# A conditioned transformer block: larger first transfers, QKV tokens by GpSimd's queue, statistics three products sooner, variances rooted later

## The chip, the cores and the metric

The kernel runs on one core of a Trainium2 chip. The metric is device time in microseconds for one execution. A core has five engines that run side by side, each through its own instructions in order: TensorE (PE) multiplies matrices, VectorE (DVE) and ScalarE (ACT) work element by element, GpSimd (POOL) does the same more slowly, and SyncE (SP) issues transfers. Transfers between main memory and the on-chip memory SBUF can be issued by SP, ACT or GpSimd. TensorE writes to PSUM, a small memory in banks.

## The reference

The block takes two rows of 2,048 tokens, 512 wide, and one condition vector for each row.

```
mod = silu(condition) @ Wada + bada          # six vectors of 512 per row
sh_a, sc_a, gt_a, sh_m, sc_m, gt_m = split(mod, 6)
xm = layernorm(x, g1, be1) * (1 + sc_a) + sh_a
q, k, v = split(xm @ Wqkv)                    # 16 heads of 32
x = x + gt_a * (softmax(causal(q k^T / sqrt(32))) v @ Wproj + bproj)
xm = layernorm(x, g2, be2) * (1 + sc_m) + sh_m
x = x + gt_m * (gelu(xm @ W1 + b1) @ W2 + b2) # hidden width 2,048
```

All of it is in 32-bit floating point.

## The kernel before

**Stages.** `dit_block_kernel` works in this order: a first stage (loads, the first modulation, the first normalized tokens); the query, key and value products of row 0 (`Qkv.run`); attention of row 0 (`attention_phase`); its output projection (`project_phase`), in which the first group of row 1 is prepared (`between`); then the same for row 1; last the MLP for both rows.

**First stage.** The condition and the scale and bias vectors (g1, be1, g2, be2, b1, b2) are loaded as rows of one tile `rows`, by ACT's queue, seven small transfers. SP's queue loads the first 512 tokens as four transfers of 256 KB (`Qkv.load_x`), two sixths of Wada as eight of 256 KB (`load_wada`), the query and key weights as four of 512 KB (`load_w`, tile `wqk`), and then the value weights (`load_wv`). TensorE transposes `rows`, and DVE copies the result to `cols`. A token's mean and variance come from DVE (`stats`, lines 216 to 221); `inv_std` turns the variances of four tiles into 1/sqrt and shift by a square root on ACT and two small operations on DVE. ACT scales the tokens in place (`scaled`, line 964), TensorE transposes them, four 128x128 blocks to a PSUM bank (line 214, tile `ps_xt`), and DVE and ACT apply the modulation on the way out of PSUM (`transposed`, result `xmT`). The modulation itself, silu(condition) @ Wada, is the matmul into `ps_mod` (`modulation`).

**Products with fewer multiplications.** Queries, keys and values are computed in groups of 512 tokens, g = 0 to 3. A product of 2 x 2 blocks is formed with seven block products in place of eight; `unit` orders them. For that, sums of weight blocks (`weight_sum`, line 944, on GpSimd in row 0) and sums of token blocks (`token_sum`, line 997, on DVE) are formed ahead. The first unit of row 0 (`plain`, tile `ps_qk`) goes without, while the weight sums are being formed. Each unit's results leave PSUM (six banks `mm`) by ACT (line 1059, 1130) and DVE (lines 1072, 1078, 1134), are split into a high and a low part (lines 1064, 1066), and are stored for attention.

**Steps inside a group.** `Qkv.run` counts 42 steps n in each group, one for each product, and prepares group g+1 at fixed steps: at n = 3 its tokens are loaded if they are not yet; at n = 10 to 13 their statistics; at 15 and 25 the scaling; at 18 and 28 the transposes; at 36 to 40 the token sums. At n = 30 the tokens of group g+2 are loaded. Between the products the first scores of attention are computed, their maxima taken by DVE (lines 498 and 504, tiles `junk`, `mx`). 

```
if n == 30 and g + 2 < NG:
    self.load_x(g + 2)
if 10 <= n < 10 + MTT and g + 1 > row.b:
    self.stats(g + 1, n - 10)
```

**MLP weights.** During both QKV stages GpSimd also forms the block sums of the MLP weights (`Pieces`, line 1253) in parts of SBUF that attention does not use yet, and stores them to main memory by its own queue (line 1273, `w1d`, `w2d`).

**What sets the order.** TensorE's instructions, and those wrapped in `act(...)` or given `keep`, keep the order of the program on their engine. All others are placed by the framework's scheduler, which may move them ahead or back on their engine by its own estimate of when their inputs are ready. Once placed, an engine executes strictly in that order. A tile with `bufs=N` has N buffers in turn: a load into it waits until the last reader of the buffer's former content is done. The transfers issued by GpSimd stand in its instruction order, among its sums.

Of the kernel before, what the change touches and what calls it, by code (L numbers as in the profile page):

```python
# [17 lines left out]
P = 128  # L18
# [9 lines left out]
def dit_block_kernel(  # L28
# [104 lines left out]


    first = const.tile([P, 1], F32, tag="first", name="first")
    nc.scalar.activation(first, eps, AF.Sqrt)


    cols = const.tile([P, 64], F32, tag="cols", name="cols")
# [60 lines left out]
    def x_rows(n):  # L200
        t0 = (n % NT) * P
        return x[n // NT, t0 : t0 + P, :]
# [695 lines left out]
    class Qkv:  # L898
# [13 lines left out]
                for n in (S1, S2, A22)  # L912
            }

        def load_x(self, g):
            xts = []
            for t in range(MTT):
                xt = self.qp.tile([P, D], F32, tag="x", name="x", bufs=4)
                nc.sync.dma_start(xt, x_rows(self.row.b * NT + g * MTT + t))
                xts.append(xt)  # L920
            self.xts[g] = xts

        def load_w(self, queue):
# [214 lines left out]
        def run(self, hp, also, early=()):  # L1138
# [3 lines left out]
            for g in range(NG):  # L1142
                at = [0]

                def tick():
# [1 line left out]
                    if n >= self.STEPS:  # L1147
                        return
                    if n == 30 and g + 2 < NG:
                        self.load_x(g + 2)  # L1150
                    if g + 1 < NG:
                        if n == 3 and g + 1 not in self.xts:
                            self.load_x(g + 1)
                        if 10 <= n < 10 + MTT and g + 1 > row.b:
                            self.stats(g + 1, n - 10)
                        if n in (15, 25):
                            self.scaled(g + 1, n // 25)
                        if n in (18, 28):
# [138 lines left out]
    def project_phase(row, psum, between):  # L1297
# [5 lines left out]
        with pool(f"proj{b}") as pp:  # L1303
# [14 lines left out]
            for k, i in enumerate(last_order):  # L1318
# [6 lines left out]
                for t in range(TQ):  # L1325
# [28 lines left out]
                        )  # L1354
                    between(n)
                    n += 1
        lo, hi = b * NT, (b + 1) * NT
        inv_std(mv2, rstd2, shift2, lo, hi)


    row = Row(0)
    with pool("wada") as wp, pool("qkv0") as qp, pool("hl0") as hp, pool(
        "ps_qkv0", bufs=6, space=PSUM
    ) as ps_mm:
        rows = wp.tile([n_rows, P], F32, tag="rows", name="rows")
        for r, n, src in (
            (0, n_cond, cond.rearrange("b (c p) -> (b c) p", p=P)),
            (r_g1, C, g1.rearrange("(c p) -> c p", p=P)),
            (r_be1, C, be1.rearrange("(c p) -> c p", p=P)),
            (r_g2, C, g2.rearrange("(c p) -> c p", p=P)),  # L1370
            (r_be2, C, be2.rearrange("(c p) -> c p", p=P)),
            (r_b1, FC, b1.rearrange("(c p) -> c p", p=P)),
            (r_b2, C, b2.rearrange("(c p) -> c p", p=P)),
        ):
            nc.scalar.dma_start(rows[r : r + n, :], src)
        wada_v = Wada.rearrange("(c p) f -> p c f", p=P)
        wada = {}

        def load_wada(s0, s1):
            w = row.vv[:, NT - 2 * C :].rearrange("p (n c) d -> p n c d", n=2)  # L1380
            if s0 % 3 == 2:
                mr = modr
            else:
                mr = wp.tile([P, D], F32, tag="mr", name="mr")
                nc.gpsimd.memset(mr, 0.0)
            for n, s in enumerate((s0, s1)):
                nc.gpsimd.dma_start(
                    mr[n * HD : n * HD + B, :],
                    bada[s * D : (s + 1) * D].partition_broadcast(B),
                )  # L1390
            for k in range(C):
                for n, s in enumerate((s0, s1)):
                    nc.sync.dma_start(w[:, n, k, :], wada_v[:, k, s * D : (s + 1) * D])
            wada[s0] = w, mr

        qkv = Qkv(row, qp, ps_mm)
        qkv.load_x(0)
        load_wada(0, 1)
        qkv.load_w(nc.sync)
        qkv.load_wv(hp, nc.sync)  # L1400

        ps_c = ps_mm.tile([P, n_rows], F32, tag="mm", name="ps_c")
        transpose(ps_c, rows)
        nc.vector.tensor_copy(cols[:, :n_rows], ps_c)
        sc = wp.tile([P, C, HD], F32, tag="sc", name="sc")
        nc.vector.memset(sc, 0.0)

        def modulation(s0):
# [7 lines left out]
            for k in range(C // 2):  # L1416
                for half in range(2):
                    for n in range(2):
                        at = (2 * half + n) * HD
                        kk = half * C // 2 + k  # L1420
                        mm(
                            ps[at : at + HD, :], sc[:, kk, :], w[:, n, kk, :],
                            start=(k == 0), stop=(k == C // 2 - 1),
# [18 lines left out]
        def scale_shift(a, c, r_g, r_be, shift, scale):  # L1442
# [6 lines left out]
                )  # L1449
            nc.vector.tensor_tensor(c, c, mod[:, shift], ALU.add)  # L1450

        for t in range(MTT):
            qkv.stats(0, t)
        halves = [qkv.norm(0, 0, True)]

        act(
            nc.scalar.activation(
                sc[:, :, :B], col(0, n_cond).rearrange("p (b c) -> p c b", c=C), AF.Silu
            )
        )  # L1460
# [15 lines left out]
        def also(g, n):  # L1476
# [52 lines left out]
    with pool("qkv1") as qp, pool("ps_qkv1", bufs=6, space=PSUM) as ps_mm:  # L1529
# [799 lines left out]
```

## Time and profile before

| | before |
|---|---|
| median of 3 runs | 2249.56 us (2248.82 to 2253.02) |
| profiled execution | 2252.46 us |
| its span | 2250.7 us |
| TensorE busy | 2210.1 us, 98% |
| VectorE busy | 1537.3 us, 68% |
| GpSimd busy | 1298.3 us, 58% |
| ScalarE busy | 1003.6 us, 45% |
| granted TensorE clock, mean | 0.999 of full speed |

The span reaches from the first to the last recorded instruction. Busy shares are averages over stages; the places that matter are found in the timeline, where an instruction's idle time before it and what released it stand in brackets. L206 is the one line through which every matmul goes, and L214 that of every transpose, so the stage is told by the tiles: `ps_qk` and `ps_a`, `ps_b`, `ps_c` are the QKV products, `ps_xt` the transposes of tokens, `s` the scores.

### The profile page before, as it was taken

What the parts mean: (1) busy time and instruction counts of PE and PEld (TensorE: products, weight loads), DVE (VectorE), ACT (ScalarE), POOL (GpSimd) and SP (SyncE); (2) the same over time, 40 slices, a digit from 0 to 9 for tenths busy, and PEclk for the clock granted to TensorE, in tenths of its full rate; (3) what the DMA queues carried; (4) which work ended last, traced back from release to release, by engine and by line L of the source; (5) the groups of instructions that cost most, each with busy time, mean ns of one, the idle gap of its engine ahead of it and who ended that gap; (6) DMA issues with size and microseconds to landing.
All of it is one profiled execution on the core that took longest, in us unless ns stands there. A gap on an engine that the chain in (4) does not pass through costs nothing.

```text
span 2250.7 us, 33467 instructions
## 1 busy us (share of the span) xinstructions
PE 2210.1 (98%) x12057; PEld 1429.4 (64%) x12057; DVE 1537.3 (68%) x3309; ACT 1003.6 (45%) x2012; POOL 1298.3 (58%) x807
## 2 busy tenths in 40 slices
PE   7999999999999999999999999999999999999998
PEld 5887555555543588855555555345787787688687
DVE  4678766777757667777677767663685585576576
ACT  4434555555564253365665556614322422331410
POOL 4253998998983696299989898444105204304210
PEclk9999999999999999999999999999999999999999
DMA  8787142231324799532324113363353354353433
GB/s 274 247 277 193 44 92 70 62 85 48 107 96 135 247 308 321 152 83 67 80 67 104 48 46 131 108 233 127 114 174 131 125 182 147 106 187 126 159 126 109
DMA packets 160510, 311.57 MB, mean 138 GB/s; under 512 B 16544, under 2 KB 48844, under 8 KB 158552
## 3 DMA queue, kind: packets, MB, share of 16 engines
q1 hardware_dynamic: 155488, 285.53, 41.8%
q0 software_dynamic: 4480, 23.36, 2.7%
q8 instruction: 95, 1.56, 0.3%
q14 instruction: 71, 0.58, 0.1%
q10 hardware_dynamic: 376, 0.55, 0.1%
HBM read 229.95 MB, written 87.29 MB: 141 GB/s over the span
## 4 chain that ended last, share of the span: by engine, by line
PE 88%; DVE 4%; POOL 3%; DMA 2%; ACT 1%; issue 1%; SPq 0%; DVEq 0%; ACTq 0%; POOLq 0%
PE ps_a L206 26%; PE st L206 18%; PE ps_b L206 12%; PE o L206 10%; PE s L206 9%; PE ps_c L206 4%; PE sm L206 3%; PE ps_o L206 3%; DVE junk L498 1%; POOL ee L695 1%; PE ps_xt L214 1%; ACT e L670 1%; DVE mx L504 1%; PE ps_o L214 1%; DVE stat L218 1%
## 5 line engine op out<-in xcount | busy, mean ns | idle before, releaser
L670 ACT ACTIVATE e<-st 128x512 f32<-128x512 f32 (+1 forms) x1152 | 575.1, 579 | 362.6 <-PE st L206 319.2
L504 DVE TENSOR_REDUCE mx<-s 128x1 f32<-128x512 f32 x576 | 381.6, 686 | 193.4 <-PE s L206 192.4
L695 POOL TENSOR_TENSOR ee<-ee,e 128x2048 f32<-128x2048 f32 x106 | 485.8, 4583 | 10.4 <-ACT e L670 4.4
L206 PE MATMUL st<-qst,kst 128*128 128x512 f32 (+3 forms) x1280 | 408.8, 386 | 0.0
L206 PE MATMUL s<-kst,qst 128*128 128x512 f32 (+3 forms) x1046 | 380.5, 395 | 6.1 <-DVE mx L504 3.7
L206 PE MATMUL ps_a<-sum,w 128*128 128x256 f32 (+1 forms) x1088 | 328.7, 431 | 0.1
L206 PE MATMUL o<-e,vv 128*32 128x512 f32 (+3 forms) x2560 | 293.2, 537 | 0.3 <-POOL e L682 0.3
L206 PEld LDWEIGHTS st<-qst,kst 128*128 128x128 f32 x1280 | 228.5, 188 | 97.7 <-issue 66.0
L498 DVE CUSTOM_DVE_ANT_0 junk<-s,causal 128x128 bf16<-128x128 f32 (+3 forms) x470 | 220.7, 470 | 61.0 <-PE s L206 47.0
L1797 POOL TENSOR_TENSOR sum<-w 128x256 f32<-128x256 f32 x30 | 22.1, 738 | 395.2 <-PE ps_a L206 263.8
L206 PEld LDWEIGHTS s<-kst,qst 128*128 128x128 f32 x1046 | 194.9, 188 | 71.1 <-DVE mx L504 17.0
L206 PEld LDWEIGHTS ps_a<-sum,w 128*128 128x128 f32 x1088 | 204.5, 190 | 40.1 <-issue 11.4
L695 POOL TENSOR_TENSOR ee<-e 128x2048 f32<-128x2048 f32 x42 | 192.5, 4583 | 43.2 <-ACT e L670 42.3
L206 PEld LDWEIGHTS <-sel 32*128 32x128 bf16 x1152 | 29.5, 91 | 197.0 <-issue 196.1
L2016 ACT ACTIVATE h<-h,cols 128x512 f32<-128x512 f32 x120 | 76.8, 711 | 136.0 <-DVE h L1718 136.0
L504 DVE TENSOR_REDUCE mx<-st 128x1 f32<-128x512 f32 x192 | 131.0, 683 | 0.6
L682 POOL TENSOR_SCALAR_AFFINE_SELECT e<-e 128x512 f32<-128x512 f32 x128 | 83.3, 669 | 67.6 <-ACT e L670 67.5
L206 PE MATMUL st<-fold,sel 32*128 32x512 bf16 (+1 forms) x1152 | 117.5, 372 | 1.3
L206 PEld LDWEIGHTS o<-e,vv 128*32 128x32 f32 x2560 | 59.1, 108 | 92.4 <-issue 73.0
L1718 DVE TENSOR_TENSOR h<-c,ps_b 128x256 f32<-128x256 f32 x90 | 37.9, 421 | 103.5 <-PE ps_b L206 103.0
L1066 POOL TENSOR_TENSOR lo<-lo,hi 128x512 fp32r<-128x512 f32 x32 | 40.6, 1274 | 103.9 <-ACT hi L1064 102.0
L206 PE MATMUL ps_b<-sum,w 128*128 128x256 f32 (+1 forms) x384 | 95.0, 383 | 0.0
(237 smaller groups left out, 3590.2 us busy)
## 6 DMA issues: line engine op xcount, KB each, us to landing
qst<-q SPq DMA_DIRECT2D x128, 256.0 KB
kst<-k SPq DMA_DIRECT2D x128, 256.0 KB
w<-w1d SPq DMA_DIRECT2D x32, 896.0 KB
w<-w2d SPq DMA_DIRECT2D x28, 1024.0 KB
w<-w2d SPq DMA_DIRECT2D x28, 768.0 KB
q<-hi SPq DMA_DIRECT2D x32, 256.0 KB
q<-lo SPq DMA_DIRECT2D x32, 256.0 KB
k<-hi SPq DMA_DIRECT2D x32, 256.0 KB
```

Source lines behind the costliest of these rows:

```text
L206: return tc.keep_in_program_order(nc.tensor.matmul(*args, **kw))
L214: return tc.keep_in_program_order(nc.tensor.transpose(dst, src, ident[:n, :n]))
L218: ins = nc.vector.bn_stats(st, xt)
L498: nc.vector.tensor_tensor_reduce(junk[:, :w], x, causal[:, QB - w :], 1.0, MASKED, ALU.add, ALU.max, m,)
L504: self.vector(nc.vector.tensor_reduce(m, x, axis=AX.X, op=ALU.max))
L670: act(nc.scalar.activation(e4[:, h, :w], sts[h][:, :w], AF.Exp))
L682: nc.gpsimd.affine_select(d, d, pattern=[[0, HC], [1, P]], compare_op=ALU.is_ge, fill=0.0, base=0, channel_multiplier=-1,)
L695: act(nc.gpsimd.tensor_tensor(dst, x, y, ALU.add))
L1066: engine.tensor_tensor(lo, d, hi.bitcast(F32), ALU.subtract)
L1718: act(nc.vector.tensor_tensor(dst, x, y, ALU.add))
L1797: act(engine.tensor_tensor(dst, u, v, op))
L2016: nc.scalar.activation(d[j], d[j], AF.Gelu, bias=col(r_b1 + half * HF + fs[j], 1))
```

## The change

1. The first transfers. Tokens come in pairs of tiles, two transfers of 512 KB for a group in place of four of 256 KB, in two buffers of a pair each in place of four. Two sixths of Wada come as four transfers of 512 KB in place of eight, each with two neighbouring 128-row blocks, and the product takes the blocks in a matching order. `rows` is split: condition, g1 and be1 are loaded first, by ACT's queue; the other four vectors by SP at step 22 of group 0 (`load_other_rows`), and are transposed and copied at step 20 of group 1 (`other_columns`). Row 0's second group of tokens is issued by SP ahead of the value weights, where it was issued at step 3.
2. The first stage's order. The first square root of a constant, which called up ACT's table, is replaced by a Silu there and a square root behind the Silu of the condition. TensorE executes 6 and 24 transposes of the identity whose result is not used (`busy`). The statistics and the scaling come after the Silu; the modulation is computed ahead of the first transposes.
3. In both rows the tokens of group g+2 are issued at step 30 by GpSimd, in place of SP.
4. The statistics of group g+1 start at step 7 in place of 10 and the first scaling at step 12 in place of 15, for g = 1 and 2; g = 0 keeps 10 and 15. Where g equals the row's number, the statistics now keep program order.
5. Row 0's square root for the second normalization, over 16 tiles, leaves the end of `project_phase` and is called at step 16 of group 0 of row 1. Row 1 keeps it in `project_phase`.

```diff
-    nc.scalar.activation(first, eps, AF.Sqrt)
...
-        def load_x(self, g):
+        def load_x(self, g, queue=nc.sync):
             xts = []
-            for t in range(MTT):
-                xt = self.qp.tile([P, D], F32, tag="x", name="x", bufs=4)
-                nc.sync.dma_start(xt, x_rows(self.row.b * NT + g * MTT + t))
-                xts.append(xt)
+            for t in range(0, MTT, 2):
+                xt = self.qp.tile([P, 2, D], F32, tag="x", name="x", bufs=2)
+                t0 = (g * MTT + t) * P
+                queue.dma_start(
+                    xt,
+                    x[self.row.b, t0 : t0 + 2 * P, :].rearrange("(n p) d -> p n d", p=P),
+                )
+                xts += [xt[:, n, :] for n in range(2)]
             self.xts[g] = xts
...
                     if n == 30 and g + 2 < NG:
-                        self.load_x(g + 2)
+                        self.load_x(g + 2, nc.gpsimd)
...
-                        if 10 <= n < 10 + MTT and g + 1 > row.b:
-                            self.stats(g + 1, n - 10)
-                        if n in (15, 25):
+                        s0 = 7 if g else 10
+                        if s0 <= n < s0 + MTT and g + 1 > row.b:
+                            self.stats(g + 1, n - s0, row.b == g)
+                        if n in (s0 + 5, 25):
                             self.scaled(g + 1, n // 25)
...
-        lo, hi = b * NT, (b + 1) * NT
-        inv_std(mv2, rstd2, shift2, lo, hi)
+        if b:
+            inv_std(mv2, rstd2, shift2, NT, 2 * NT)
...
-        rows = wp.tile([n_rows, P], F32, tag="rows", name="rows")
-        for r, n, src in (
+        rows = [
+            wp.tile([n, P], F32, tag=f"rows{n}", name="rows")
+            for n in (r_g2, n_rows - r_g2)
+        ]
+        parts = (
...
-            nc.scalar.dma_start(rows[r : r + n, :], src)
+        for r, n, src in parts[:3]:
+            act(nc.scalar.dma_start(rows[0][r : r + n, :], src))
+        act(nc.scalar.activation(first, eps, AF.Silu))
+
+        def load_other_rows():
+            for r, n, src in parts[3:]:
+                nc.sync.dma_start(rows[1][r - r_g2 : r - r_g2 + n, :], src)
+
+        def other_columns():
+            ps = ps_sp.tile([P, n_rows - r_g2], F32, tag="s", name="ps_c")
+            transpose(ps, rows[1])
+            nc.vector.tensor_copy(cols[:, r_g2:n_rows], ps)
...
-            for k in range(C):
+            for k in range(0, C, 2):
                 for n, s in enumerate((s0, s1)):
-                    nc.sync.dma_start(w[:, n, k, :], wada_v[:, k, s * D : (s + 1) * D])
+                    nc.sync.dma_start(
+                        w[:, n, k : k + 2, :], wada_v[:, k : k + 2, s * D : (s + 1) * D]
+                    )
...
         qkv.load_w(nc.sync)
+        qkv.load_x(1)
         qkv.load_wv(hp, nc.sync)
 
-        ps_c = ps_mm.tile([P, n_rows], F32, tag="mm", name="ps_c")
-        transpose(ps_c, rows)
-        nc.vector.tensor_copy(cols[:, :n_rows], ps_c)
+        ps_w = ps_sp.tile([P, P], F32, tag="s", name="ps_w")
+
+        def busy(n):
+            for _ in range(n):
+                transpose(ps_w, ident)
+
+        busy(6)
+        ps_c = ps_sp.tile([P, r_g2], F32, tag="s", name="ps_c")
+        transpose(ps_c, rows[0])
...
-                        kk = half * C // 2 + k
+                        kk = 2 * k + half
...
+        act(
+            nc.scalar.activation(
+                sc[:, :, :B],
+                ps_c[:, :n_cond].rearrange("p (b c) -> p c b", c=C), AF.Silu,
+            )
+        )
+        act(nc.scalar.activation(first, eps, AF.Sqrt))
+        nc.vector.tensor_copy(cols[:, n_cond:r_g2], ps_c[:, n_cond:])
+        busy(24)
         for t in range(MTT):
             qkv.stats(0, t)
-        halves = [qkv.norm(0, 0, True)]
...
+        qkv.scaled(0, 0)
+        qkv.scaled(0, 1)
         picks()
         columns = modulation(0)
+        halves = [qkv.norm(0, 0, True)]
+        columns()
         halves.append(qkv.norm(0, 1, True))
-        columns()
...
                 load_wada(2, 5)
+                load_other_rows()
+            elif (g, n) == (1, 20):
+                other_columns()
...
+            elif (g, n) == (0, 16):
+                inv_std(mv2, rstd2, shift2, 0, NT)
             pieces.tick()
```

More of the change, by code (lines that the diff above doesn't have):

```diff
@@ L1373, in dit_block_kernel @@
             (r_b2, C, b2.rearrange("(c p) -> c p", p=P)),
-        ):
-            nc.scalar.dma_start(rows[r : r + n, :], src)
+        )
[9 more added lines that the diff above has]
+            nc.vector.tensor_copy(cols[:, r_g2:n_rows], ps)
         wada_v = Wada.rearrange("(c p) f -> p c f", p=P)
@@ L1450, in scale_shift @@
             nc.vector.tensor_tensor(c, c, mod[:, shift], ALU.add)
+        act(
[3 more added lines that the diff above has]
+            )
+        )
+        act(nc.scalar.activation(first, eps, AF.Sqrt))
+        nc.vector.tensor_copy(cols[:, n_cond:r_g2], ps_c[:, n_cond:])
+        busy(24)
         for t in range(MTT):
             qkv.stats(0, t)
-        halves = [qkv.norm(0, 0, True)]
[L1456 to L1460, printed above, removed]
+        qkv.scaled(0, 0)
+        qkv.scaled(0, 1)
         picks()
         columns = modulation(0)
+        halves = [qkv.norm(0, 0, True)]
+        columns()
         halves.append(qkv.norm(0, 1, True))
-        columns()
         scale_shift(a1, c1, r_g1, r_be1, 0, 1)
```

## The prediction

> **What bounds the kernel now.** I read the page first, then the timeline of the first stage, the stretches of its loads, the waits around the token statistics, and the same places in the second row.
>
> ```profile
> span 2250.7 us, 33467 instructions
> ...
> PE 2210.1 (98%) x12057; PEld 1429.4 (64%) x12057; DVE 1537.3 (68%) x3309; ACT 1003.6 (45%) x2012; POOL 1298.3 (58%) x807
> ```
>
> TensorE is busy for 98% of the span. Some 40 us of idle time is all that can be won, and a microsecond in which TensorE newly waits is lost for good. The profiled execution took 2252.46 us, 2.9 above the median of 2249.56; each term below is a difference read from that execution, and I add their sum to the median. 0.2% of it, 4.5 us, is about what a measurement can tell from no change.
>
> In the timeline the columns are start, length, engine, line, operation, tiles, count, and in brackets the idle time before with what ended it.
>
> ```profile
> 18.28 8.83 PE L206 MATMUL ps_qk<-xmT,wqk 128*128 128x512 f32 x16 [1.78 <-DVE xmT L269]
> ...
> 19.08 10.52 POOL L944 TENSOR_TENSOR wqk<-wqk 128x256 f32<-128x256 f32 x12 [0.67 <-DMA wqk<-in_L_cond_Wqkv_dram]
> ...
> 29.72 1.10 PE L206 MATMUL ps_a<-t,wqk 128*128 128x256 f32 x4 [0.89 <-POOL wqk L944]
> ```
>
> The wait of the first stage that ends last is at 29.72: GpSimd can start its twelve weight sums only when the last QKV weight lands (19.08), needs 10.52 us, and TensorE waits for them. So the start is worth what the landing of these weights is worth.
>
> **The start: fewer, larger transfers.** The last number of each stretch is GB/s.
>
> ```profile
> 2.00:9.00 7.00, 0.30 (x1) 0.18 (x1) 4.13 (x16) 2.45 (x4) 3.40 (x8) 1.00 0.88 275
> 9.00:13.60 4.60, 4.17 (x23) 2.35 (x24) 0.00 (x0) 3.75 (x6) 0.00 (x0) 1.00 1.00 353
> 13.60:19.10 5.50, 3.72 (x23) 2.38 (x21) 3.15 (x10) 1.23 (x3) 1.57 (x4) 1.00 1.06 389
> ...
> 20.00:22.00 2.00, 2.00 (x4) 0.88 (x3) 1.97 (x3) 0.00 (x0) 2.00 (x3) 0.50 1.09 366
> ```
>
> 275 x 7.0 + 353 x 4.6 + 389 x 5.5 make 5.69 MB by 19.1 us. At 389 throughout they take 14.6 us instead of 17.1, a gain of 2.5; at 353 throughout, 1.0. Twelve transfers of tokens and Wada become six, and the row loads that the first stage does not need go to step 22 of group 0, so the queue has its bytes earlier; I take -2.5, range -1 to -4 (if the sums on GpSimd, with less beside them, also run quicker). The activation tables called up in another order, 30 dummy transposes and a Wada product in another order lie beside this wait: nothing, while it ends last. If that cover goes, the cold clock is the price: 0.50 of full speed in the last row, after the 1.78 us of idle time, which is 1 us in two. The four row loads, one transpose and one copy in later groups are under 0.2 us together.
>
> **Statistics.** From group 1 on they move from step 10 to step 7, the square root and first scalings with them.
>
> ```profile
> 80.42 0.33 PE L214 MATMUL ps_xt<-ident,x 128*128 128x128 f32 x1 [1.01 <-ACT x L964]
> 81.13 0.98 PE L214 MATMUL ps_xt<-ident,x 128*128 128x128 f32 x7 [0.38 <-ACT x L964]
> ...
> 829.15 0.33 PE L214 MATMUL ps_xt<-ident,x 128*128 128x128 f32 x1 [0.56 <-ACT x L964]
> 829.86 0.98 PE L214 MATMUL ps_xt<-ident,x 128*128 128x128 f32 x7 [0.38 <-ACT x L964]
> ```
>
> These waits of the transposes for the scaled tokens go: -1.4 in row 0, -0.9 in row 1. Group 0 of row 0 gets the reverse: before, the scheduler ran its statistics seven microseconds early, as soon as the tokens had landed; now they are held in program order at steps 10 to 13, with square root and scalings behind. Nothing before shows that; its nearest row is the one at 80.42, the same chain at the same steps, so +1.5 (0.5 to 2).
>
> **Tokens by GpSimd's queue, row 0.** What a late load costs, and what such a load takes, in the timeline and in the list of transfers (KB each, median us from issue to landing):
>
> ```profile
> 115.92 0.69 DVE L218 BATCH_NORM_STATS2 stat<-x 128x6 f32<-128x512 f32 x1 [1.57 <-DMA x<-in_x_dram]
> ...
> 117.26 1.92 PE L206 MATMUL ps_mod<-vv,sc 128*32 128x512 f32 x16 [0.95 <-DVE mx L504]
> ```
> ```profile
> wqk<-in_L_cond_Wqkv_dram POOLq DMA_DIRECT2D x4, 512.0 KB, 8.7
> w2d<-vv POOLq DMA_DIRECT2D x10, 448.0 KB, 6.0
> ```
>
> VectorE works in order. A statistic whose tokens are late stops it (1.57), what is queued behind it waits, and TensorE loses 0.95. This load leaves SP's queue, where it stood behind others, and is early now: -0.95.
>
> But the scheduler moves statistics ahead of their step on VectorE, to where it believes the tokens landed. In the changed order the first of group 2 stands right behind the copy at 41.27, the last of group 3 behind the mask at 95.23; their buffers come free with the transposes at 38.92 and 91.10:
>
> ```profile
> 38.92 1.04 PE L214 MATMUL ps_xt<-ident,x 128*128 128x128 f32 x8
> ...
> 41.27 0.41 DVE L1078 TENSOR_TENSOR lo<-lo,ps_a 128x256 f32<-128x256 f32 x1
> ...
> 91.10 1.04 PE L214 MATMUL ps_xt<-ident,x 128*128 128x128 f32 x8
> ...
> 95.23 0.43 DVE L498 CUSTOM_DVE_ANT_0 junk<-s,causal 128x256 bf16<-128x256 f32 x1 [2.13 <-PE s L206]
> ```
>
> So 1.7 and 4.1 us lie between release and need, and a load of this size takes 6.0 to 8.7: VectorE stands for 2 to 7 us at each of four such loads, of which TensorE's six PSUM banks hide a part. I take +1 each, +4 together (0, all hidden, to 10).
>
> **Row 1.** Here GpSimd itself is in the way. It has to issue the loads, in order with the sums of the MLP weights and their stores, and it is busy without a break:
>
> ```profile
> 812.60 10.79 POOL L1253 TENSOR_TENSOR vv<-vv 128x512 f32<-128x512 f32 x9
> 823.34 0.56 POOL L1273 DMA_DIRECT2D w2d<-vv  x1
> ...
> 842.54 2.09 POOL L1253 TENSOR_TENSOR qst<-qst 128x256 f32<-128x256 f32 x3
> 844.58 0.56 POOL L1273 DMA_DIRECT2D w2d<-kst  x1
> ...
> 848.59 1.61 POOL L1273 DMA_DIRECT2D w2d<-qst  x3
> ```
>
> Before, SP has issued these tokens by 816.59 and 860.62. In the changed order on GpSimd the second pair of group 2 stands behind the sums that end at 823, the first pair of group 3 behind those that end at 845, the second behind the last stores, at 852. With the 6.0 of the stores, the nearest row in queue and place, they land at 829, 851 and 858; with 8.7, at 832, 854 and 861. VectorE and TensorE before:
>
> ```profile
> 821.17 1.09 DVE L1066 TENSOR_TENSOR lo<-lo,hi 128x512 fp32r<-128x512 f32 x1
> ...
> 834.75 0.68 DVE L498 CUSTOM_DVE_ANT_0 junk<-s,causal 128x512 bf16<-128x512 f32 x1
> ...
> 839.17 0.42 DVE L1078 TENSOR_TENSOR lo<-lo,ps_a 128x256 f32<-128x256 f32 x1 [0.44 <-PE ps_a L206]
> ...
> 845.00 0.42 DVE L1134 TENSOR_TENSOR vv<-vv,ps_b 128x256 f32<-128x256 f32 x1
> ```
> ```profile
> 825.55 1.89 PE L206 MATMUL ps_a<-t,wqk 128*128 128x256 f32 x8
> ...
> 841.80 1.03 PE L206 MATMUL ps_a<-t,wqk 128*128 128x256 f32 x4
> ...
> 848.32 1.89 PE L206 MATMUL ps_a<-wv,t 128*128 128x256 f32 x8
> ```
>
> In the changed order the statistics of these three pairs stand behind the work at 821.17, behind the mask at 834.75 and before the sum at 845.00. Queued behind each are the sums that empty PSUM and the halves to be stored; ScalarE's square root waits for the statistics too, with copies out of PSUM behind it. TensorE runs on with what banks it has, to 825.55, 841.80 and 848.32.
>
> - Second pair of group 2: 829 + 4.3 (3.4 from 822.2 to 825.55 as before, and a second statistic with its aggregate, 0.9) - 825.55 = 8.
> - First pair of group 3: VectorE's own work from 835.4 to 839.6 adds up to 3.0, two statistics and aggregates to 1.7: 851 + 4.7 - 841.8 = 14. It holds the 8 already; the two are not added.
> - Second pair of group 3: 858 + 2.6 (statistics 1.7, two sums of 0.42) - 848.3 = 12, hidden behind the 14; with 8.7, 15.
>
> I take +14 from the 6.0, and +1 for the clock after such a pause: +15. Bounds: the quickest store in the group took 3.1 us, which makes 11 of the 14; a gain is excluded, since nothing waits for these tokens before beyond the 0.9; the longest took 10.3, which makes 18.
>
> ```profile
> DMA to landing us min/median/max: 3.1/6.3/10.3
> ```
>
> If GpSimd's own sums had slack that I don't see and the loads went out ahead of them, the term is 0; I keep that as a rival.
>
> The Trainium skill, "DMA: Bandwidth & Descriptors", section "Anatomy of one DMA — SWDGE (gpsimd) path", gives about 2.0 us plus the bytes at 436 GB/s for a transfer issued by GpSimd, an estimate of 3.2 us for 512 KB. The 8.7 and 6.0 above contradict it as they stand, though those transfers had others beside them. By that rule the row 0 term would be 0 and row 1 11 + 1, which is the second rival's 2257.
>
> **The variances** of the second normalization leave the end of row 0's projection for step 16 of row 1.
>
> ```profile
> 774.83 0.31 ACT L224 ACTIVATE rstd<-mv,eps 128x16 f32<-128x16 f32 x1 [7.74 <-DVE mv L221]
> ...
> 775.46 1.13 PE L206 MATMUL ps_a<-t,wqk 128*128 128x256 f32 x4 [2.36 <-ACT lo L1059]
> ```
>
> In the changed order this square root still stands ahead of the same copies on ScalarE: the scheduler draws it back, as its inputs are ready. The 2.36 stays, so 0 (at best -2.0).
>
> **Sum**: -2.5 start, -1.4 and -0.9 waits gone, +1.5 group 0, -0.95 late load gone, +4 row 0, +15 row 1, 0 variances = +14.8, so 2249.56 + 14.8 = 2264.
>
> **Rivals.**
> - The loads arrive in time (the other side). For it: row 0 has GpSimd idle there, and if the two GpSimd loads of row 1 go out within 3 us of their release, nothing waits. Without the +4 and +15: -4.3, so 2245; with the variances, 2243. It decides where the second-to-last load lands before 841.8 - 4.7 = 837, 14 us sooner than I place it. Against it: the unbroken sums at 812 to 850. Chance 0.14, split between faster (0.08) and same (0.06): half the start's gain suffices for same.
> - The loads land as fast as the quickest store, in 3.1 us, each going out with little beside it: row 0 at 0 and row 1 at its 11 + 1 give +7.7, 2257; if only the second pair of group 2 bites, +8 + 1 gives 2254. For it: these tokens come one or two transfers at a time, the four of 8.7 together. Against it: the median of ten stores, 6.0. Chance 0.20, nearly all slower (0.02 same).
> - All loads late by the longest store, 10.3 us: row 0 at +10, row 1 at 18 + 1 give +24.8, 2274. For it: the 8.7 of the tokens' own size. Against it: the banks of PSUM, and the median. Chance 0.12.
> - The change doesn't do what it says: the variances are drawn back, above, and that is in the sum.
>
> My forecast has 0.54. Faster 0.08, same 0.08, slower 0.84. The range: from 2250, which leaves out most of the first rival, to 2277, a little past the third rival's time.
>
> **What would show it.** Right: on VectorE, statistics at about 822, 835 and 845 that wait 6 us or more for the tokens; on GpSimd, token loads issued at about 823, 845 and 852; TensorE gaps of about 8 and 6 us in 825 to 850; the 29.72 moved to about 27; no wait at 80.42 and 117.26; a gap of about 1.5 at the transposes of group 0; the 2.36 still there. Wrong: if those loads land under 3 us after issue, if GpSimd issues them before the sums, or if TensorE finds other matmuls to run while VectorE stands.

## The result, and the profile after

The changed kernel takes 2280.12 us (2279.44 to 2281.45, 4 runs) against 2250.07 (2248.82 to 2253.02, 4 runs) beside it: slower by a factor of 1.0129, with a 95% interval of 1.0114 to 1.0145, 30.0 us. I had forecast 2264 and a range to 2277. The direction was right, the size only half.

The profiled execution took 2279.99 us, its span is 2278.0: 27.3 us more than the span before (that execution took 2252.46, 2.4 above the median beside the result). Cut at the same seven products of TensorE, the two spans compare stretch by stretch. The columns are the stretch, its length, TensorE's busy time and matmuls, its granted clock, the share of the DMA engines and GB/s. Before:

```profile
0.00:29.72 29.72, 17.94 (x65) 0.94 0.87 288
29.72:117.26 87.54, 83.72 (x408) 1.00 0.82 252
...
734.00:775.46 41.46, 38.70 (x106) 1.00 0.71 238
775.46:823.00 47.54, 47.54 (x230) 1.00 0.89 286
823.00:870.20 47.20, 45.33 (x218) 1.00 1.00 334
870.20:900.00 29.80, 28.79 (x141) 1.00 0.94 304
```

After:

```profile
0.00:26.35 26.35, 20.83 (x95) 1.00 0.92 313
26.35:127.33 100.98, 87.62 (x411) 0.97 0.75 235
...
744.80:784.25 39.45, 38.23 (x105) 1.00 0.74 247
784.25:831.80 47.55, 47.55 (x230) 1.00 0.88 278
831.80:894.60 62.80, 49.76 (x218) 0.86 0.79 272
894.60:927.10 32.50, 30.04 (x143) 0.95 0.76 249
```

So the start gives 3.4, row 0's QKV stage loses 13.4, the turn of the rows gives 2.0, and row 1's QKV stage loses 15.6 and 2.7; the stretches left out (all attention and the MLP) differ by 0.9 together. Each loss has two parts. In row 0 TensorE's idle time grows by 9.5 us (100.98 - 87.62 against 87.54 - 83.72), and its busy time by 3.9 for the same work; in row 1's first stretch it is 11.2 and 4.4. Where the busy time grows, the clock is below 1.

The idle time begins on VectorE. Its timeline after, the statistics that waited in brackets:

```profile
45.26 1.29 DVE L217 BATCH_NORM_STATS2 stat<-x 128x6 f32<-128x512 f32 x2 [6.35 <-DMA x<-in_x_dram]
...
57.71 0.69 DVE L217 BATCH_NORM_STATS2 stat<-x 128x6 f32<-128x512 f32 x1 [6.01 <-DMA x<-in_x_dram]
...
95.61 1.29 DVE L217 BATCH_NORM_STATS2 stat<-x 128x6 f32<-128x512 f32 x2 [5.41 <-DMA x<-in_x_dram]
...
105.60 0.69 DVE L217 BATCH_NORM_STATS2 stat<-x 128x6 f32<-128x512 f32 x1 [3.14 <-DMA x<-in_x_dram]
...
839.74 0.69 DVE L217 BATCH_NORM_STATS2 stat<-x 128x6 f32<-128x512 f32 x1 [7.68 <-DMA x<-in_x_dram]
...
861.83 1.29 DVE L217 BATCH_NORM_STATS2 stat<-x 128x6 f32<-128x512 f32 x2 [8.41 <-DMA x<-in_x_dram]
```

From the view of the token tile `x`, the sum of these stops (with 3.3 us at the kernel's very first tokens, which every version has) and the time from issue to landing of the loads by GpSimd:

```profile
  DVE stat L217: 40.3, 8
...
DMA to landing us min/median/max: 4.8/8.5/8.9
```

TensorE runs on for a while on what its PSUM banks allow, then stops, and starts again at half clock: the eight matmuls at 59.12 and at 843.17 take 3.78 us, where the same eight took 1.89 before (the second of them is the 825.55 of the prediction).

```profile
59.12 3.78 PE L205 MATMUL ps_a<-wv,t 128*128 128x256 f32 x8 [4.49 <-DVE vv L1137]
...
784.25 1.13 PE L205 MATMUL ps_a<-t,wqk 128*128 128x256 f32 x4 [0.67 <-ACT lo L1062]
...
843.17 3.78 PE L205 MATMUL ps_a<-t,wqk 128*128 128x256 f32 x8 [8.66 <-DVE lo L1081]
...
864.51 2.07 PE L205 MATMUL ps_b<-wv,t 128*128 128x256 f32 x4 [4.39 <-DVE lo L1075]
...
919.75 0.47 PE L205 MATMUL s<-kst,qst 128*128 128x512 f32 x1 [2.46 <-issue]
```

GpSimd issued row 1's loads here:

```profile
822.41 0.73 POOL L919 DMA_DIRECT2D x<-in_x_dram  x1
...
831.07 0.72 POOL L919 DMA_DIRECT2D x<-in_x_dram  x1
...
855.50 0.73 POOL L919 DMA_DIRECT2D x<-in_x_dram  x1
...
861.82 0.72 POOL L919 DMA_DIRECT2D x<-in_x_dram  x1
```

The second lands at 839.7, 8.7 us after its issue, and VectorE had stood at the first statistic that needs it since 832.1.

The start, after:

```profile
17.66 7.13 PE L205 MATMUL ps_qk<-xmT,wqk 128*128 128x512 f32 x16 [0.85 <-DVE xmT L268]
```
```profile
17.87 10.48 POOL L947 TENSOR_TENSOR wqk<-wqk 128x256 f32<-128x256 f32 x12
```
```profile
26.35 1.03 PE L205 MATMUL ps_a<-t,wqk 128*128 128x256 f32 x4
```

GpSimd's weight sums begin 1.2 us sooner. The product that waited at 29.72 before starts at 26.35 without a wait, 2.0 us before the twelve sums end (28.35), so it does not need them all. TensorE's own first product is now what ends last, 1.7 us shorter at full clock (7.13 against 8.83).

### The profile page after: what moved, and what is told of

It reads as the page before. It is cut to its first block, busy times and chain, and to the rows that moved or that the text cites. A ratio compares the mean times of both kernels' runs of the same rounds, so it can differ in the third digit from the quotient of the medians.

```text
span 2278.0 us, 33486 instructions
## 1 busy us (share of the span) xinstructions
PE 2222.1 (98%) x12088; PEld 1440.7 (63%) x12088; DVE 1531.1 (67%) x3310; ACT 1003.1 (44%) x2012; POOL 1303.7 (57%) x815
## 4 chain that ended last, share of the span: by engine, by line
PE 85%; POOL 4%; DVE 4%; DMA 2%; issue 1%; ACT 1%; SPq 0%; DVEq 0%; ACTq 0%; POOLq 0%
PE ps_a L205 24%; PE st L205 18%; PE ps_b L205 11%; PE o L205 10%; PE s L205 9%; PE ps_o L205 4%; PE sm L205 3%; PE ps_c L205 3%; DMA x<-in_x_dram 1%; POOL ee L694 1%; DVE junk L497 1%; POOL kst L1257 1%; PE ps_xt L213 1%; ACT e L669 1%; DVE mx L503 1%
```

## The experiments

Each run is compared with the kernel before on the same chip (medians of 2250.07 to 2252.19 us there). Differences of medians in us, with the ratio and its 95% interval:

| run | us | ratio |
|---|---|---|
| the change | +30.0 | 1.0129 (1.0114 to 1.0145) |
| SP's queue in both rows | +3.2 | 1.0016 (1.0007 to 1.0025) |
| the queue alone | +42.5 | 1.0188 (1.0172 to 1.0203) |
| SP in row 0 | +18.8 | 1.0087 (1.0070 to 1.0104) |
| SP in row 1 | +12.4 | 1.0052 (1.0038 to 1.0066) |
| statistics held | +9.7 | 1.0049 (1.0034 to 1.0064) |
| held, row 1 issued early | +4.2 | 1.0015 (1.0006 to 1.0024) |
| held, SP in row 1 | +2.6 | 1.0013 (1.0004 to 1.0022) |
| the same, variances held | +0.9 | 1.0004 (0.9995 to 1.0013) |
| the first stage alone | +10.8 | 1.0049 (1.0036 to 1.0061) |
| SP, no dummy transposes | +3.5 | 1.0013 (1.0003 to 1.0022) |
| SP, nothing held | +4.3 | 1.0018 (1.0009 to 1.0027) |
| mixed | +6.3 | 1.0025 (1.0014 to 1.0035) |
| mixed, single transfers in row 1 | -2.7 | 0.9988 (0.9979 to 0.9997) |
| first stage, single transfers | +1.0 | 1.0004 (0.9994 to 1.0013) |

### Is it the queue?

The theory: late token loads by GpSimd's queue stop VectorE. The rival: the statistics three products sooner stop it, whichever queue loads.

```diff
-                        self.load_x(g + 2, nc.gpsimd)
+                        self.load_x(g + 2)
```

> The changed kernel with the tokens of group g+2 issued by SP again; the rest of the change is kept. Theory A (the time goes into late token loads: each of the eight loads by GpSimd lands 5 to 9 us after its issue, VectorE stands for it, 40.3 us in all): the row 0 term of +13 and the row 1 term of +18 go, what is left is the start (-3.4), group 0's held statistics (+2.1), the waits gone (-0.8, -0.9) and the row turn (-2.1): 2243 to 2249. Rival B (it is the earlier step of the statistics that makes VectorE stop, whichever queue issues the loads): 2262 to 2282. The same 512 KB by SP's queue should land in under 5 us after issue by theory A.

Measured: +3.2 us. VectorE's stops for tokens, the first ones included, fall from 40.3 us to 5.3, and some 27 of the 30 us go with the queue. The rival falls. The expected gain of 1 to 7 us on before did not come either, which led to the runs on the first stage below. The eight loads, now SP's, took 4.3 to 7.9 us from issue to the last increment of their semaphore, so "under 5" held for three of them only.

Then the queue by itself, in the kernel before:

```diff
-                        self.load_x(g + 2)
+                        self.load_x(g + 2, nc.gpsimd)
```

> The kernel before with one edit: the tokens of group g+2 (four loads of 256 KB) are issued by GpSimd. Theory A: slower by most of the 31 us of the two rows, 2268 to 2285. Rival B: within 5 us of before, 2247 to 2255. Four smaller loads cost GpSimd four issues in place of two, but each lands sooner; by that alone up to 8 us less than the whole.

Measured: +42.5 us, above what was expected: four issues instead of two go through GpSimd, and VectorE stops twelve times for 60.2 us in all (2.3 of it at the kernel's first tokens). The longest stop on VectorE, and TensorE's wait behind it, in the timelines of this run:

```profile
825.36 0.69 DVE L218 BATCH_NORM_STATS2 stat<-x 128x6 f32<-128x512 f32 x1 [16.56 <-DMA x<-in_x_dram]
```
```profile
835.55 3.55 PE L206 MATMUL ps_a<-wv,t 128*128 128x256 f32 x8 [18.57 <-DVE vv L1134]
```

So the queue costs 42.5 us by itself and 30.0 - 3.2 = 26.8 with the rest of the change around it: the rest softened its cost, it did not make it.

### Which row?

```diff
-                        self.load_x(g + 2, nc.gpsimd)
+                        self.load_x(g + 2, nc.gpsimd if row.b else nc.sync)
```

> The changed kernel with SP for the tokens of group g+2 in row 0 alone; row 1 keeps GpSimd. Theory A: row 0's +13 goes, row 1's +18 stays, 2264 to 2269, with the two stops of 7.7 and 8.4 us on VectorE in row 1 unchanged. If the rows help one another (a late row 0 making room in row 1), it is outside that.

The other way round:

```diff
-                        self.load_x(g + 2, nc.gpsimd)
+                        self.load_x(g + 2, nc.sync if row.b else nc.gpsimd)
```

> The changed kernel with SP for the tokens of group g+2 in row 1 alone; row 0 keeps GpSimd, its statistics placed freely as in the change. The counterpart of the run with SP in row 0: if the two rows' losses are independent, row 0's stops (6.4, 6.0, 5.4 and 3.1 us on VectorE) put it 10 to 12 us behind at 730 us, and it ends 10 to 14 us slower than before. If a late row 0 makes room in row 1, under 9.

Measured: +18.8 with SP in row 0, 2 us above the expected, with stops of 7.4 and 5.0 us on VectorE in row 1; and +12.4 with SP in row 1, as expected. The two are nearly independent: 18.8 + 12.4 - 3.2 (neither) = 28.0 against 30.0 (both). Row 0's queue costs 12.4 - 3.2 = 9.2 us, row 1's 15.6.

### Late loads, or statistics placed too soon?

In VectorE's order in the traces, the first statistic of row 0's group 2 is instruction 57 with GpSimd's queue and instruction 93 with SP's: the scheduler places it by its own estimate of the landing. Held in program order, it is instruction 77.

```diff
-                            self.stats(g + 1, n - s0, row.b == g)
+                            self.stats(g + 1, n - s0, True)
```

> The changed kernel, GpSimd's queue and all, with every statistic of groups 1 to 3 held in program order (steps 7 to 10) and not only those where the group equals the row. Theory A1 (the loads are late only because the scheduler places the statistics soon after it believes the tokens landed; some eight places further back nothing would wait): row 0's +13 goes to under 2, row 1's second stop (8.4 us) shrinks by half or more, its first (7.7 us, already held) stays: 2258 to 2267. Theory A2 (the loads are too late for any place that the steps allow): 2275 to 2282.

Measured: +9.7 us, 20 less than the change, with the same loads on the same queue, whose median is still 7.6 us from issue to landing. All of row 0's loss is gone (its QKV stage ends 1.9 us ahead of before), and of row 1's the second stop. So two thirds of the loss was the place of the statistics in VectorE's order. What stays is in the main one wait of TensorE, with the half clock behind it:

```profile
831.15 3.78 PE L205 MATMUL ps_a<-t,wqk 128*128 128x256 f32 x8 [7.49 <-DVE lo L1081]
```

It is the second pair of row 1's group 2, whose statistics the change held already. If GpSimd's place for the issue is its cause, issuing it earlier among the sums removes it. A third pair of buffers allows that:

```diff
-                xt = self.qp.tile([P, 2, D], F32, tag="x", name="x", bufs=2)
+                xt = self.qp.tile([P, 2, D], F32, tag="x", name="x", bufs=2 + self.row.b)
...
-                    if n == 30 and g + 2 < NG:
+                    if n == (19 if row.b else 30) and g + 2 < NG:
```

> The held kernel, GpSimd's queue in both rows, but in row 1 a third pair of token buffers and the loads of group g+2 at step 19, so that GpSimd reaches them 10 to 20 us sooner among its sums. Theory (row 1's 9.7 us come from where the loads stand among GpSimd's sums, not from the queue's own time to land): the stop of 7.7 us on VectorE and the one after it go, and the kernel lies within 3 us of before. Rival (GpSimd's loads are late by nature, or disturb its sums): 6 us or more slower than before, as the held kernel was (9.7).

Measured: +4.2 us. GpSimd now issues row 1's four loads here:

```profile
748.52 0.75 POOL L919 DMA_DIRECT2D x<-in_x_dram  x1
...
802.07 0.72 POOL L919 DMA_DIRECT2D x<-in_x_dram  x1
825.09 0.72 POOL L919 DMA_DIRECT2D x<-in_x_dram  x1
845.70 0.72 POOL L919 DMA_DIRECT2D x<-in_x_dram  x1
```

VectorE waits for no token any more after the first, though the median from issue to landing is still 7.4 us, and the wait of 7.49 is gone. The expected 3 us were missed by a little: smaller waits came up (3.0 at 837, 3.3 at 899), of the kind that the next runs are about.

### Why is the start's gain not kept?

The held kernel with SP's queue in row 1, as an edit of the changed kernel:

```diff
-                        self.load_x(g + 2, nc.gpsimd)
+                        self.load_x(g + 2, nc.sync if row.b else nc.gpsimd)
...
-                            self.stats(g + 1, n - s0, row.b == g)
+                            self.stats(g + 1, n - s0, True)
```

> The changed kernel with all statistics held in program order, GpSimd's queue for the tokens of row 0 and SP's for those of row 1. Theory: row 0 loses nothing by GpSimd's queue once the statistics stand later (in the held kernel it stood 2 us ahead of before at 730 us), and row 1 loses nothing with SP's: 2 us ahead of before, give or take 1.5. If GpSimd's queue had a price of its own in row 0, or the earlier step in row 1, it is no faster than before.

Measured: +2.6 us, where 2 less than before were expected. In its profile row 0's QKV stage ends 3.8 us ahead of before, nearly all of the start's gain, and row 1 gives 5.4 back, most of it at 825 to 830. Then the variances, their square root held in program order:

```diff
-        nc.scalar.activation(rstd[:, lo:hi], mv[:, lo:hi, 1], AF.Sqrt, bias=eps)
+        act(nc.scalar.activation(rstd[:, lo:hi], mv[:, lo:hi, 1], AF.Sqrt, bias=eps))
```

> The kernel of the run above with the square root of the variances held at its place in the program, so that it really stands at step 16 of row 1 and not ahead of the first copies out of PSUM. The wait at the turn of the rows (2.36 us before, 1.6 to 1.9 with the variances where the scheduler puts them) shrinks under 0.7: 1 to 2 us faster than the run above. Rival: the copies there wait for GpSimd's and DVE's tokens anyway and the wait stays, no difference.

Measured: +0.9 us, 1.6 less than the run above, as expected in size, though the intervals overlap. The turn of the rows gains 2.8 us in the profile, and it is lost again at 826.

One thing more is seen in this profile, of an execution 2.8 us above its median. The order in row 0 is that of the run above, and yet row 0 loses 4.5 us more, from 101 us on. A subtraction on VectorE takes 3.06 us in place of 1.13, and GpSimd's sums beside it begin at 101.91 where they began at 99.90. Its row in the run above, in this one, and the sums of this one:

```profile
101.42 1.13 DVE L1069 TENSOR_TENSOR lo<-lo,hi 128x512 fp32r<-128x512 f32 x1
```
```profile
101.49 3.06 DVE L1069 TENSOR_TENSOR lo<-lo,hi 128x512 fp32r<-128x512 f32 x1
```
```profile
101.91 3.23 POOL L1257 TENSOR_TENSOR qst<-qst 128x256 f32<-128x256 f32 x4
```

So a loss of this size at one place can come and go between two executions with the same order of instructions, and what the runs below lose at single places in one profile has to be read with that.

The first stage alone, with SP's queue, step 10, nothing held, and the variances in their old place:

```diff
-                        self.load_x(g + 2, nc.gpsimd)
+                        self.load_x(g + 2)
...
-                        s0 = 7 if g else 10
+                        s0 = 10
...
-                            self.stats(g + 1, n - s0, row.b == g)
+                            self.stats(g + 1, n - s0)
...
-        if b:
-            inv_std(mv2, rstd2, shift2, NT, 2 * NT)
+        inv_std(mv2, rstd2, shift2, b * NT, (b + 1) * NT)
...
-            elif (g, n) == (0, 16):
-                inv_std(mv2, rstd2, shift2, 0, NT)
```

> The first stage of the change alone (pairs, Wada in four, condition first, the 30 transposes, the second group of tokens ahead of the value weights); SP's queue, statistics at step 10 placed freely, variances at the end of the projection. The start gave 3.4 to 3.9 us in every run so far and the held statistics of group 0, absent here, took 1 to 2 back: 2.5 to 4 us faster than before. If the earlier second group costs the value weights, under 2.

Measured: +10.8 us, the opposite sign. The first stage gives its 4.4 us, and then the token preparation and the scores beside it give back 19, of which smaller gains on the way return 4: 0.9 at 31 us, 2.6 at 78 to 84, 5.1 at 106 to 111, 4.6 at 813 to 835, 6.0 near 900. Without the dummy transposes, the run with SP's queue else:

```diff
-        busy(6)
...
-        busy(24)
```

> The changed kernel with SP's queue for all tokens (the first run) and without the 30 transposes of the identity. Theory (they keep the clock at full speed into the first products; GpSimd's weight sums end last all the same): the first product on summed weights, which the first run had at 25.86 us, stays within 0.5 us, since GpSimd and not TensorE sets it. Rival (the start's gain of 3.9 us is in part the warm clock): it comes 1 to 2 us later, at 27 to 28, with a granted clock under 0.95 in the first 26 us as in the kernel before (0.94).

Measured: +3.5, and the product that waited at 29.72 before (called the first on summed weights there) at 26.22 us against 25.86, with the granted clock at 1.00 in the first 26 us either way. The transposes do next to nothing here. With no statistic held, again in the run with SP's queue:

```diff
-                            self.stats(g + 1, n - s0, row.b == g)
+                            self.stats(g + 1, n - s0)
```

> The first run's kernel (SP's queue) with no statistic held in program order, in group 0 of row 0 and group 1 of row 1 neither. If holding them costs what the waits at the transposes of group 0 show (1.0 to 2.1 us in the runs so far), those waits go and the first row stands 1 to 2 us further ahead at 60 us than in the first run (which had -2.9 there). Rival: the scheduler's free places serve no better, no difference.

Measured: +4.3, against +3.2 with them held: no gain. The wait at group 0's transposes goes, and one of 0.72 us at 27.61 takes its place. At 60 us TensorE stands 1.3 us further ahead than in the run with SP's queue, as expected, and by 870 it stands 1.1 behind it.

Then the best part of each, row 0 held on GpSimd's queue, row 1 as before on SP's at step 10, the variances held:

```diff
-                        s0 = 7 if g else 10
+                        s0 = 7 if g and not row.b else 10
...
-                            self.stats(g + 1, n - s0, True)
+                            self.stats(g + 1, n - s0, not row.b)
```

> Row 0 as in the held kernel (GpSimd's queue, step 7, statistics held), row 1 as before the change (SP's queue, step 10, statistics placed freely), and the variances' square root held at step 16. Row 0 gave 4 us by 730 us with that, the turn of the rows 1.5 to 2.5, and row 1 should give nothing back: 3 to 6 us faster than before. Rival (whatever is gained early is given back in the second row, where VectorE and GpSimd meet): within 2 us of before.

Measured: +6.3 us, where 3 to 6 less than before were expected. Its profile, of an execution 2.9 us above the median, stands 4.9 us ahead after the turn of the rows and loses 8.0 by 870, most of it at 830, and 5.7 near 900. The loss at 830 is one small instruction on VectorE. Its timeline and GpSimd's and TensorE's at that place:

```profile
825.50 4.13 DVE L225 SCALAR_TENSOR_TENSOR shift<-mv,rstd 128x4 f32<-128x4 f32 x1
```
```profile
825.90 1.27 POOL L1257 TENSOR_TENSOR kst<-kst,qst 128x512 f32<-128x512 f32 x1
827.12 1.27 POOL L1257 TENSOR_TENSOR qst<-kst 128x512 f32<-128x512 f32 x1
828.34 1.26 POOL L1257 TENSOR_TENSOR kst<-kst 128x512 f32<-128x512 f32 x1
```
```profile
830.53 0.47 PE L213 MATMUL ps_xt<-ident,x 128*128 128x128 f32 x1 [5.00 <-ACT x L967]
```

At most of its other places this 128x4 operation takes 0.14 to 0.28 us. Here it lasts until GpSimd's third sum ends (829.60), ScalarE's scaling waits for it, and the transposes for that. What moved it there may be that a pair lands as one. The last two runs go back to single transfers into the same pair buffers, in row 1 of the mixed kernel, and in all later groups of the first-stage kernel (there with `if g or self.row.b:`):

```diff
-                queue.dma_start(
-                    xt,
-                    x[self.row.b, t0 : t0 + 2 * P, :].rearrange("(n p) d -> p n d", p=P),
-                )
+                src = x[self.row.b, t0 : t0 + 2 * P, :].rearrange("(n p) d -> p n d", p=P)
+                if self.row.b:
+                    for n in range(2):
+                        queue.dma_start(xt[:, n, :], src[:, n, :])
+                else:
+                    queue.dma_start(xt, src)
```

> The mixed kernel with row 1's tokens loaded as four transfers of 256 KB again (into the same pair buffers). Theory P (row 1 gave the gain back because a pair lands as one, 1 to 3 us after single tiles did, which moved the shift of VectorE under three sums of GpSimd): the 5.0 us wait at the transposes near 830 us goes and the run is 3 to 6 us faster than before. Theory C (VectorE and GpSimd meet at some place in any case, where the first stage's gain has moved the one against the other): a wait of 2 to 5 us stays somewhere between 820 and 900 us and it is no faster than before.

> The run with the first stage alone (11 us slower than before), with the tokens of all later groups as transfers of 256 KB again. Theory P: its losses at 82 us, at 106 to 112, at 812 to 835 and at 893 us go, and the 4.4 us of the start are kept: 3 to 4.5 us faster than before. Theory C: the places change and at least half of the 15 us given back in that run stays: 3 us or more slower than before.

Measured: -2.7 and +1.0 us. Against the same kernels with pairs that is 9.0 and 9.8 us. The wait of 5.00 is 0.88, and the shift takes 0.16:

```profile
822.80 0.16 DVE L225 SCALAR_TENSOR_TENSOR shift<-mv,rstd 128x4 f32<-128x4 f32 x1
```
```profile
824.25 0.33 PE L213 MATMUL ps_xt<-ident,x 128*128 128x128 f32 x1 [0.88 <-ACT x L969]
```

Neither theory's numbers came out: by P both were to be 3 us or more faster than before, by C neither was to be faster. What is shown is that in these two kernels one transfer of 512 KB is worse than two of 256 KB, by 9 to 10 us. That it is so because a pair lands as one is not shown, since a second thing changed with it: the scheduler placed other instructions elsewhere. With single transfers the square root on ScalarE and the shift on VectorE stand further ahead in their engines' orders, and the shift is done at 822.96, when GpSimd runs no sum. The loss near 900 is one of order. In the mixed kernel GpSimd forms the low half of one key tile only after its sums, as the first of four. Its store goes out at 892.27 on SP's queue, the loads of the queries for the scores stand behind it, and the scores wait:

```profile
890.96 4.97 POOL L1069 TENSOR_TENSOR lo<-lo,hi 128x512 fp32r<-128x512 f32 x4
```
```profile
892.27 0.34 SPq L1034 DMA_DIRECT2D k<-lo  x1
892.66 2.54 SPq L359 DMA_DIRECT2D qst<-q  x2
```
```profile
900.62 0.77 PE L205 MATMUL s<-kst,qst 128*128 128x512 f32 x1 [4.62 <-DMA qst<-q]
```

With single transfers the same low half stands among the sums, as it did before the change (878.93), and this loss is gone:

```profile
875.61 1.27 POOL L1071 TENSOR_TENSOR lo<-lo,hi 128x512 fp32r<-128x512 f32 x1
```

The first-stage kernel with single transfers still gives back about 3 of its 4 us, in steps of 1 to 2. The mixed kernel with single transfers is the only one here that is faster than before; 0.12% is less than the 0.2% that I called measurable, though its interval excludes 1.

## Why the prediction was right and wrong

- **The start, -2.5.** Measured -3.4: near in size, but by luck, for I read the wait at 29.72 wrongly. I put it down to GpSimd's twelve sums, which end at 29.60. By the program this product needs only the third of them, done at 22.58; in the changed kernel it starts before the twelve have ended. It also needs ScalarE's copy of the bank `ps_a`, to which it adds, and in the kernel before that copy stood behind a table load and the square root of group 1's variances:

```profile
27.76 1.28 ACT L224 ACT_TABLE_LOAD   x1
29.06 0.30 ACT L224 ACTIVATE rstd<-mv,eps 128x4 f32<-128x4 f32 x1
29.26 0.36 ACT L1059 ACTIVATE lo<-ps_a 128x256 f32<-128x256 f32 x1
```

  The copy ends at 29.62, just after the last sum, and TensorE starts. In the changed kernel neither stands there, and the copy ends at 26.07. In the run with the first stage alone the square root is ahead of the copy again, but no table load, and the product waits for nothing. So the other order of the tables, which I put at nothing, is enough to take this wait away. Of the 3.4 us, 0.6 are the earlier first tokens (18.28 to 17.66), 1.7 the first product at full clock, and 1.1 this wait. I had written the clock down as a price only if the cover went.
- **Statistics, -1.4, -0.9 and +1.5.** The waits at 80.42 and 829 went and gave 1.5 and 1.3, the one at 117.26 gave 0.9. Holding group 0 cost 1.6 at its transposes, near the forecast. Letting it go gave 1.3 back at 60 us, which was lost again in row 1.
- **Tokens in row 0, +4. This step failed.** I had the stops on VectorE right ("2 to 7 us at each of four such loads"; 6.4, 6.0, 5.4 and 3.1), and then took 1 us each because "TensorE's six PSUM banks hide a part". The first stop was hidden but for about 1; behind the others TensorE lost 7, 2 and 4 us, the clock included: 14 in place of 4. (By the runs, row 0's queue costs 9.2 us, and nothing once the statistics are held.) Nothing quoted showed how much the banks hide; a ratio was there, 1.57 on VectorE to 0.95 on TensorE, and by it 20.9 us of stops give 12.6.
- **Landing.** I took the 6.0 of the stores as nearest "in queue and place". The loads took 8.5 in the median, near the 8.7 of the row of their own size and direction.
- **Tokens in row 1, +15.** The mechanism was right: GpSimd's issues at 831.07, 855.50 and 861.82 and the stops on VectorE came where they were forecast, shifted by row 0's loss, and TensorE's two waits add up to 13.05 us against the 14. The terms beside it were mis-sized: the clock cost 4.4 us in the first stretch where I took 1, and the late scores (2.46 and their clock) were not foreseen.
- **The clock in general.** I priced it at 1 us. Over the QKV stages TensorE's busy time for the same work grew by 3.9 + 4.4 + 1.3 = 9.6 us, a third of the result. The Trainium skill, "TensorE: Matmul & The Clock Gate", section "What's actually happening", says that after an idle window of about 3.4 us the array runs at half clock until it has been busy for about as long; the 1.89 us that became 3.78 behind the 4.49 and 8.66 us waits agree with it. The length of one wait does not tell it alone: the kernel before ran at 0.50 of full speed from 19.5 to 22.9 us, soon after a wait of 1.78 us, and the changed kernel stayed at full clock after waits of 1.98 and 1.79 us at 99 and 108.
- **The variances, 0.** The square root stands where it stood, as forecast, but the wait behind it fell from 2.36 to 0.67, with the sums on the projection's tokens ahead of it less late: VectorE waited 2.44 us for GpSimd's before the last of them, and 1.80 for TensorE's product now. Held at its step, in three runs, the wait went to nothing and the turn gave 2.0 to 2.8: a little more than the "at best -2.0", which the change reached without holding it, though not as I thought.
- **The rivals.** "The loads arrive in time" fell. The rule of about 2.0 us plus the bytes (the Trainium skill, "DMA: Bandwidth & Descriptors", section "Anatomy of one DMA — SWDGE (gpsimd) path") would make 3.2 us, an estimate; the fastest of the eight loads took 4.8, the median 8.5. The third rival, all loads late, was the nearest with 2274. It too had the banks and the clock wrong.

## What to carry to other kernels

A load that moves to another queue, or is cut into other sizes, also moves whatever the scheduler places by its estimate of that load's landing. Look where the consumers now stand: holding them back gave 20 of the 30 us here, with the loads as late as before. On an engine that works in order, take a stop of several microseconds as mostly lost unless a row shows it hidden (here 20.9 us of stops in row 0 cost 14, the half clock included), and take the time to land from the row of the same size and direction. And where a wait is put down to one engine, check in the program that the instruction needs the result that ended there: another may have ended at the same moment.

## What the runs showed of the hardware

- Loads of 512 KB issued by GpSimd took 7.1 to 8.9 us to land in row 0 of the changed kernel, and 4.8 to 8.7 in row 1 (median of all 8.5). The same eight by SP's queue took 4.3 to 7.9. How much of the difference is the queue and how much other transfers was not separated.
- An operation of VectorE on two operands in SBUF can stand while GpSimd runs sums. A 128x4 operation that takes 0.14 to 0.28 us at most places took 4.13, until the third of three GpSimd sums had ended; the sums followed one another without a break until 829.60, and it ended at 829.63. In the run with the variances held, the first break of the sums comes at 103.99, and the subtraction of 3.06 us ends at 104.55. The Trainium skill, "GPSIMD Engine Reference", section "Key points", names this sharing for VectorE's instructions with two SBUF inputs; the 4.13 is what it can cost one of them. Whether it strikes depends on shifts of a microsecond or two. This may be why gains at the start came and went in these runs; that it explains each of them was not shown.
